# Joining blocks of 32-column matmuls in a planned two-layer transformer kernel, with an earlier start and an earlier first expert weight

## The chip, the cores and the metric

The kernel runs on one core of a Trainium2 chip. The metric is the device time of one execution in microseconds (us). The engines are named as in the profile: PE is TensorE (PEld its weight loads), DVE is VectorE, ACT is ScalarE, POOL is GpSimd, SP is SyncE, which here issues most of the DMAs.

## The reference

32 sequences of 128 tokens with 512 channels pass through two layers; `cond` gives one vector for each sequence. Everything is float32. Layer 0 is attention with 16 heads of 64 (wide: 1024 channels in all), a routing in which each of 8 experts picks its best 512 tokens of the 4096, and the experts' MLP (2048 wide). Layer 1 is attention with 16 heads of 32 and a plain MLP. Cut to what matters here:

```python
# layer 0
shift = silu(t) @ W_ada.T
h = ln(x) + shift
q, k, v = split(h @ Wqkv.T)            # q and k normed per head
o = softmax(q k^T / 8) v
x = x + o @ Wout.T
tok = x.reshape(-1, d)
gate = softmax(tok @ Wgate.T)          # 4096 x 8
vals, idx = top_k(gate.T, 512)         # per expert
y = gelu(ln(tok[idx]) @ fc1[e].T) @ fc2[e].T * vals
tok = tok.at[idx].add(y)
# layer 1
normed = adaln(x, cond)
x = x + attention(normed) @ wo.T
x = x + gelu(adaln(x, cond) @ w1.T) @ w2.T
```

## The kernel before

`fast_kernel` is one program for all of it (a second, general one stands behind it for inputs that don't fit its assumptions and doesn't run here). It does not issue instructions as it goes through the code. Each piece of work is given to a planner with `sch.op(engine, estimated us, function, w=writes, r=reads, prio, job, ...)`: an *operation*, which may be one instruction or a whole block of them. When all are known, `Sched.run` sets the order: again and again it takes the operation that can start earliest by its own estimates, and among equals the one with the lowest `prio`. A window of three jobs is open at a time. Each engine then issues its operations in that order, with waits where the data needs them. So a different estimate or one operation less can move others; `lat` is the estimated time to landing of a DMA, and `share` scales the estimated size of one.

Buffers come from pools: `row` (tiles in SBUF, the on-chip memory), `weight` (weight tiles there), `bank` (PSUM, where PE writes; eight).

- **Start.** SP issues the DMAs of `prm` (columns of parameters), `cT` (the condition), `wg` (gate weights), then the first two sequences `x` (`load_x`, L1165), `wada` (`load_w`, L1122) and six `wqkv`. ACT loads its table and makes `sT` of `cT` (L1189). DVE norms x (L336 to L339, then `xn` L1411), PE transposes it (`tpx` L1113) and multiplies `sT` with `wada` (`pa` L1197); ACT copies that (`zs_a` L1128), PE adds it up (`pu_a` L1201), DVE makes `hshift` (L1205) and `hT` (L1419), and the first projection (`pq` L1305) begins.
- **Layer 0**, `pair(g)` for 16 pairs of sequences (L1288). q, k and v come from products of half matrices in which seven products take the place of eight (`seven`, matmuls at L1346, form 128*128, a full PE array). Then `back(b, i, ...)` does the attention of sequence i of the pair: transposes of q and k (`tpq`), scores (`sc`, L1469, form 64*128), exps on ACT (`pe`, L1475), row sums of the exps with a matrix of ones (`ps`, L1485, form 128*32: the array is split into four strips of 32 columns), the outputs (`po`, L1491, form 128*32) and `oT` = `po` times the reciprocal of the sums (L1498). Ln, Exp and two DVE operations make the reciprocal (`recip`). After that the gates' logits: `gates` (L1519, form 128*32) sums `xT` times `wg` (4 matmuls) and `oT` times `ww` (8) in four strips of `pgz` (the profile counts each float32 matmul as two instructions: x8 and x16); a copy `zg`, and a small matmul `pg` with `sel` (L1523, 8 columns wide) adds the strips up. DVE copies `pg` to `lg`. `project` (L1557) multiplies `oT` with `wout`, and SP stores the result to `tok` and to `acc` in DRAM (`send`, L1579). The last 16 sequences (`LATE`) put `oT` into DRAM, and their projection (`late_projection`) comes while the routing searches its thresholds.
- **Routing and experts.** `expert_tokens` makes the list of tokens of each expert (`oh` L1712, `pi` L1732). `expert(e, after)` gathers the tokens (`xg`, POOL's indirect DMA, L1776), norms, transposes (`tpg`) and multiplies them with `fc1` (u, L1885), again with seven products for eight, for which DVE sums halves of the tokens (`tg`, L1137) and POOL halves of the weights (`s`, L1138; four sums for each of four tiles m of fc1). The tiles m = 2 and 3 of expert 0, and its fc2, wait for a small DMA, `fence`, that reads the last gathered token (L1782).
- **Layer 1**, `group(g)` for 16 groups of two sequences: transposes of the normed x (`a_..t`), q, k and v (L2251, L2297), and for each sequence the scores (`quads`, L2347, form 32*128), the exps (L2350), the row sums (`sums`, `ps`, L2358, form 128*32), the outputs (`outs`, `po`, L2364, form 128*32) and `oT`. Then the output projection (`o`, L2297) and the MLP, up (`m`, L2425) and down (`n`, L2486). PE's gaps in the attention of a group are filled with the MLP of the group before.

The lines that the change touches in `back`, cut:

```python
sch.op(PE, mm_us(D), sums, w=[ps], r=pe[0] + pe[1], prio=pa + 3, job=job)
...
pgt = pb + 41
...
sch.op(PE, mm_us(S, len(parts) // DC), gates, w=[pz], r=need, prio=pgt, job=job)
copy([zs], [pz], lambda: zs.t, lambda: pz.t, S, pgt, job)
```

and in `group`:

```python
sch.op(PE, mm_us(D), sums, w=[ps], r=pe, prio=pa + 5, job=job)
sch.op(PE, mm_us(S, 4), outs, w=[po], r=pe + [v[i]], prio=pa + 5, job=job)
```

## Time and profile before

| what | us |
|---|---|
| median of 3 runs (3240.48 to 3243.26) | 3242.57 |
| the profiled execution | 3242.52 |
| its span | 3240.5 |
| PE busy in it (share of the span) | 3199.2 (99%) |
| start, to the first `tpx` | 10.42 |
| layer 0 (to 960, the start in it) | 960 |
| routing and late projection | 126 |
| expert 0 until PE is busy again throughout (1086 to 1126) | 40 |
| the rest of the experts (to 1935) | 809 |
| layer 1 (to the end) | 1305 |

The stages are read from the trace by the lines that run in them. The first lines of the profile's page, below its sum of busy times, cut the span into 40 slices and give the busy tenths of each (9 is 90% or more) and the granted clock of PE in tenths of full speed:

```profile
PE   8999999999999899999999999999999999999999
DVE  7877776878677787756665547666666666666665
PEclk9999999999999899999999999999999999999999
```

PE's row is below 9 in the first slice (the start) and in the slice that holds the change from routing to expert 0, and PE's clock is lower there too. A line of the timeline reads: start in us, duration in us, engine, line, operation, output<-inputs, form of the array (for PE), shape, type, number of instructions, and in brackets the idle time before and what ended it. The ends of matmuls are modelled; their starts are recorded, so distances of starts are the better measure.

### The profile page before, as it was taken

The page shows a single profiled execution, that of the slowest core. Times are in us where ns is not written, and L with a number is a line of the kernel's source. Part 1 is how long each engine was busy: PE and PEld are TensorE (multiplying, and loading weights), DVE is VectorE, ACT ScalarE, POOL GpSimd, SP SyncE. Part 2 cuts the span into 40 slices and gives each one's busy share as a digit, 9 for nine tenths or more (in the row PEclk, how much of TensorE's full clock was granted, in tenths as well). Part 3 has the DMA queues.
Part 4 walks back from the last instruction along what each step waited for, and adds up shares of the span by engine and source line. Part 5 has one row for each costly group of instructions (what it writes and reads, how often), then busy time and mean ns, then how long its engine had stood idle before and what let it go on. Part 6 is the DMA issues. An engine that isn't in the chain of part 4 may idle for free. (4 is left out here: it accounts for less than half of the span.)

```text
span 3240.5 us, 55814 instructions
## 1 busy us (share of the span) xinstructions
PE 3199.2 (99%) x21786; PEld 2559.9 (79%) x21786; DVE 2242.1 (69%) x4854; ACT 959.7 (30%) x2302; POOL 705.3 (22%) x557
## 2 busy tenths in 40 slices
PE   8999999999999899999999999999999999999999
PEld 4665666555557688888888888999999999999998
DVE  7877776878677787756665547666666666666665
ACT  3333333344431122221222213333333333333332
POOL 0111111000023458766676510000000000000000
PEclk9999999999999899999999999999999999999999
DMA  4122112222125523444333463333333333333343
GB/s 173 53 78 67 63 57 76 91 83 66 51 88 195 160 86 103 119 112 116 101 103 99 146 202 103 99 99 101 100 102 102 101 102 99 98 100 101 103 137 105
DMA packets 247122, 335.39 MB, mean 103 GB/s; under 512 B 22082, under 2 KB 156738, under 8 KB 246338
## 3 DMA queue, kind: packets, MB, share of 16 engines
q1 hardware_dynamic: 239394, 314.30, 29.9%
q0 software_dynamic: 7168, 16.91, 2.8%
q8 instruction: 174, 2.85, 0.4%
q14 instruction: 98, 0.80, 0.1%
q10 hardware_dynamic: 288, 0.52, 0.1%
HBM read 277.01 MB, written 54.66 MB: 102 GB/s over the span
## 5 line engine op out<-in xcount | busy, mean ns | idle before, releaser
L2372 POOL TENSOR_TENSOR hi_t<-hi_t,inv 128x512 f32<-128x512 f32 x32 | 40.8, 1273 | 1223.7 <-DVE inv L1148 1223.7
L2436 ACT ACTIVATE m<-m,prm 128x128 f32<-128x128 f32 x512 | 162.0, 389 | 236.7 <-DVE m L2430 236.2
L1949 PE MATMUL d<-fc,h 128*128 128x256 f32 x992 | 218.9, 380 | 0.0
L1949 PEld LDWEIGHTS d<-fc,h 128*128 128x128 f32 x992 | 188.4, 190 | 24.9
L1896 ACT ACTIVATE h<-h,prm 128x256 f32<-128x256 f32 x256 | 114.9, 500 | 259.3 <-DVE h L1890 259.2
L1885 PE MATMUL u<-gT,fc 128*128 128x256 f32 x768 | 180.4, 386 | 0.8 <-ACT gT L1852 0.8
L1885 PEld LDWEIGHTS u<-gT,fc 128*128 128x128 f32 x768 | 148.6, 194 | 21.9 <-ACT gT L1852 1.2
L2430 DVE TENSOR_TENSOR m<-mu,m 128x512 f32<-128x512 f32 x128 | 87.9, 688 | 108.1 <-PE m L2425 105.2
L1312 ACT ACTIVATE sq<-qk 128x512 f32<-128x512 f32 x128 | 80.7, 632 | 232.1 <-DVE qk L1350 227.9
L2430 DVE TENSOR_TENSOR mu<-mu,m 128x512 f32<-128x512 f32 x96 | 65.9, 687 | 87.1 <-PE m L2425 87.1
L2425 PE MATMUL m<-n2a,w_s 128*128 128x128 f32 x1024 | 125.0, 276 | 0.0
L1885 PE MATMUL u<-tg,s 128*128 128x256 f32 x512 | 121.8, 381 | 2.2 <-DVE tg L1137 2.2
L2486 PE MATMUL n<-w_t,m 128*128 128x256 f32 x512 | 123.0, 380 | 0.0
L1890 DVE TENSOR_TENSOR h<-v,u 128x512 f32<-128x512 f32 x128 | 86.7, 683 | 52.0 <-PE u L1885 50.3
L2425 PE MATMUL m<-n2T,w 128*128 128x128 f32 x1024 | 119.7, 275 | 0.0
L2425 PEld LDWEIGHTS m<-n2a,w_s 128*128 128x128 f32 x1024 | 119.5, 192 | 0.0
L2425 PEld LDWEIGHTS m<-n2T,w 128*128 128x128 f32 x1024 | 118.2, 192 | 0.8
L2486 PE MATMUL n<-w_t,ms 128*128 128x256 f32 x512 | 117.6, 383 | 0.0
L1346 PE MATMUL q<-wqkv,hT 128*128 128x512 f32 x240 | 114.6, 608 | 0.5 <-DVE oT L1498 0.4
L2486 PE MATMUL n<-w,m 128*128 128x256 f32 x512 | 114.7, 383 | 0.0
L1346 PE MATMUL q<-wqkv,hsb 128*128 128x512 f32 x240 | 114.0, 597 | 0.1
L1949 PE MATMUL d<-t,hs 128*128 128x256 f32 x512 | 113.5, 379 | 0.0
(1193 smaller groups left out, 7492.3 us busy)
## 6 DMA issues: line engine op xcount, KB each, us to landing
w_t<-t2d SPq DMA_DIRECT2D x256, 256.0 KB, 3.2
w<-in_w_dram SPq DMA_DIRECT2D x192, 256.0 KB, 4.5
fc<-in_fc_dram SPq DMA_DIRECT2D x64, 512.0 KB, 4.7
fc<-in_fc_dram SPq DMA_DIRECT2D x32, 1024.0 KB, 5.6
x<-in_x_dram SPq DMA_DIRECT2D x32, 256.0 KB, 3.3
xT<-in_xT_dram SPq DMA_DIRECT2D x32, 256.0 KB, 2.7
otd<-oT SPq DMA_DIRECT2D x32, 256.0 KB, 2.1
ol<-otd SPq DMA_DIRECT2D x32, 256.0 KB, 3.7
```

Source lines behind the costliest of these rows:

```text
L1312: sch.op(ACT, act_us(D), lambda: nc.scalar.activation(sq.t, qk[i][j].t, AF.Square), w=[sq], r=[qk[i][j]], prio=pr, job=job)
L1346: nc.tensor.matmul(ps[m].t, lhs()[:, k, :], rhs[0](k), start=(k == 0), stop=(k == 1))
L1885: nc.tensor.matmul(ps[n].t[:, t, :], lhs()[:, k, t * P : (t + 1) * P], rhs.t[:, k, :], start=(k == 0), stop=(k == 1))
L1890: sch.op(DVE, dve_us(D), lambda: nc.vector.tensor_tensor(o_.t, a_.t, ps[n].t, ALU.add), w=[o_], r=[a_, ps[n]], prio=pr, job=job)
L1896: sch.op(ACT, act_us(HQ, 1), lambda t=t, c=c: nc.scalar.activation(o_.t[:, t, :], o_.t[:, t, :], AF.Gelu_apprx_tanh, bias=col("b1s", e * 1 ...
L1949: nc.tensor.matmul(ps[n].t[:, j, :], lhs[m].t[:, k, t * P : (t + 1) * P], rhs.t[:, 2 * m + k, :], start=(m == 0 and k == 0), stop=(m == NM ...
L2372: sch.op(POOL, pool_us(D), lambda inv=inv: nc.gpsimd.tensor_tensor(hi_b.t, hi_b.t, flat(inv), ALU.add), w=[hi_b], r=[inv], prio=pr + 197, ...
L2425: nc.tensor.matmul(ps[n].t[:, u, :], l1w[what].t[:, k, (NQ * q + u) * P : (NQ * q + u + 1) * P], rhs()[:, k, :], start=(k == 0), stop=(k = ...
L2430: sch.op(DVE, dve_us(D), lambda: nc.vector.tensor_tensor(o_.t, a_.t, ps[n].t, ALU.add), w=[o_, *more], r=[a_, ps[n]], prio=pq_, job=job)
L2436: sch.op(ACT, act_us(S, 1), lambda u=u, c=c: nc.scalar.activation(o_.t[:, u, :], o_.t[:, u, :], AF.Gelu, bias=col("b1", c), scale=1.0), w= ...
L2486: nc.tensor.matmul(ps[n].t, Ah[lhs][c // NQ].t[:, c % NQ, :], b_.t[:, k, :], start=(c == 0), stop=(c == 7))
```

## The change

- `prm`, `cT` and `wg` are loaded by DMAs that ACT issues instead of SP. `load_w` takes a `share`, 0.6 for `wada`, which makes the planner expect it earlier.
- In layer 0 the gates of the first sequence of a pair are no longer an operation of their own: `back` returns them as `ahead`, and they stand in one operation with the row sums of the second sequence, directly before these. The gates of the second sequence stay alone. `zg` and `pg` hold both sequences: the two small matmuls are one operation, and one DVE copy makes `lg` in place of two.
- In layer 1 the row sums and outputs of both sequences of a group are one PE operation.
- The acc stores of the last pair wait until both tok stores have landed.
- fc1's tiles 2 and 3 of expert 0 no longer wait for the fence.

```diff
@@ -1048,9 +1048,9 @@
         return const.tile(list(shape), dtype, name=name)
 
     prm = const_tile("prm", (P, NCOL))
-    nc.sync.dma_start(prm, cols)
+    nc.scalar.dma_start(prm, cols)
     cT = const_tile("cT", (P, DC, NB))
-    nc.sync.dma_start(cT, condT.rearrange("(k p) b -> p k b", p=P))
+    nc.scalar.dma_start(cT, condT.rearrange("(k p) b -> p k b", p=P))
     ident = const_tile("ident", (P, P))
     make_identity(nc, ident)
     ones_f = const_tile("ones_f", (P, 64))
@@ -1095,7 +1095,7 @@
 
     wg = const_tile("wg", (P, DC, 32))
     nc.vector.memset(wg, 0.0)
-    nc.sync.dma_start(wg[:, :, :E], wgate.rearrange("(k p) e -> p k e", p=P))
+    nc.scalar.dma_start(wg[:, :, :E], wgate.rearrange("(k p) e -> p k e", p=P))
     ww = const_tile("ww", (P, 8, 32))
     nc.vector.memset(ww, 0.0)
     wg_b, ww_b = stands(wg), stands(ww)
@@ -1116,12 +1116,12 @@
 
         return a.unsqueeze(2).to_broadcast([a.shape[0], a.shape[1], n])
 
-    def load_w(src, k0, n0, name, prio, job, lat=6.5, spare=0, r=()):
+    def load_w(src, k0, n0, name, prio, job, lat=6.5, spare=0, r=(), share=1.0):
 
         b_ = weight(name)
         sch.op(SP, 0.06, lambda: nc.sync.dma_start(
             b_.t, src[k0 : k0 + 512, n0 : n0 + 512].rearrange("(k p) n -> p k n", p=P)),
-            w=[b_], r=r, lat=lat, prio=prio, job=job, spare=spare)
+            w=[b_], r=r, lat=lat, prio=prio, job=job, spare=spare, share=share)
         return b_
 
     def copy(w, r, out_, src, n, pr, job, first=ACT):
@@ -1166,7 +1166,7 @@
 
     load_x(0)
     load_x(1)
-    wada_b = load_w(w_ada, 0, 0, "wada", -300, 0, 9.0)
+    wada_b = load_w(w_ada, 0, 0, "wada", -300, 0, 9.0, share=0.6)
 
     wqkv_b = {}
     for i, j in enumerate((4, 5, 0, 2, 1, 3)):
@@ -1381,7 +1381,10 @@
             sch.op(DVE, 0.19, lambda i=i: nc.vector.tensor_scalar(var[i].t, var[i].t, 1.0 / HD0, EPS, ALU.mult, ALU.add),
                    w=[var[i]], r=[var[i]], prio=pp + 10 + 100 * i, job=job)
             rs = st.newton(var[i], 2 * H0, f"qk_{b0 + i}", pp + 10 + 100 * i, job)
-            oT.append(back(b0 + i, i, job, lg, qk[i], v[i], rs))
+            if i == 0:
+                zs, ahead = row(f"zg_{g}", (P, 2, S)), None
+            oT_, ahead = back(b0 + i, i, job, lg, qk[i], v[i], rs, zs, ahead)
+            oT.append(oT_)
         if b0 >= NB - LATE:
             late_projection(g)
         else:
@@ -1424,7 +1427,7 @@
 
         return hT
 
-    def back(b, i, job, lg, qk, v, rs):
+    def back(b, i, job, lg, qk, v, rs, zs, ahead):
         pb = b * 100.0
         pp = pb - 50
         xt = x_b[b]
@@ -1490,7 +1493,15 @@
                     d0 = (2 * t + r) * HD0 + 32 * i
                     nc.tensor.matmul(po[i].t[g : g + 32, t, :], v[half].t[:, d0 : d0 + 32], pe[half][r].t[:, t, :],
                                      start=True, stop=True)
-        sch.op(PE, mm_us(D), sums, w=[ps], r=pe[0] + pe[1], prio=pa + 3, job=job)
+        if i == 0:
+            sch.op(PE, mm_us(D), sums, w=[ps], r=pe[0] + pe[1], prio=pa + 3, job=job)
+        else:
+
+            def gates_sums(gates0=ahead[0]):
+                gates0()
+                sums()
+            sch.op(PE, mm_us(S, 3) + mm_us(D), gates_sums, w=[ps, ahead[1]], r=pe[0] + pe[1] + ahead[2], prio=pa + 3, job=job)
+            copy([(zs, 0)], [ahead[1]], lambda: zs.t[:, 0, :], lambda p_=ahead[1]: p_.t, S, pa + 3, job)
         inv = row(f"inv_{b}", (P, 4, S))
         recip(inv, ps, pa + 4, job)
         for o_, p_, fn in zip(oT, po, (lambda: outs(0), lambda: outs(1))):
@@ -1510,7 +1521,7 @@
         parts = [(wg, k, xt_T, k) for k in range(DC)] + [(ww, k, oT[k // 4], k % 4) for k in range(8)]
         need = [xt_T, wg_b, ww_b] + oT
         pgt = pb + 41
-        pz, zs, pg = bank(f"pgz_{b}", (P, S)), row(f"zg_{b}", (P, S)), bank(f"pg_{b}", (P, E))
+        pz = bank(f"pgz_{b}", (P, S))
 
         def gates(pz=pz):
             n = len(parts) // DC
@@ -1518,17 +1529,21 @@
                 g = q % DC
                 nc.tensor.matmul(pz.t[32 * g : 32 * g + 32, :], w_[:, k, :], src.t[:, kk, :],
                                  start=(q < DC), stop=(q >= (n - 1) * DC))
-        sch.op(PE, mm_us(S, len(parts) // DC), gates, w=[pz], r=need, prio=pgt, job=job)
-        copy([zs], [pz], lambda: zs.t, lambda: pz.t, S, pgt, job)
-        sch.op(PE, mm_us(E), lambda: nc.tensor.matmul(pg.t, zs.t, sel[:, :E], start=True, stop=True), w=[pg], r=[zs, cst_b],
-               prio=pgt, job=job)
-        sch.op(DVE, 0.16, lambda: nc.vector.tensor_copy(lg.t[:, i * E : (i + 1) * E], pg.t), w=[(lg, i)], r=[pg],
-               prio=pgt, job=job)
+        if i:
+            pg = bank(f"pg_{b}", (P, 2, E))
+            sch.op(PE, mm_us(S, len(parts) // DC), gates, w=[pz], r=need, prio=pgt, job=job)
+            copy([(zs, 1)], [pz], lambda: zs.t[:, 1, :], lambda: pz.t, S, pgt, job)
+
+            def add_up():
+                for n in range(2):
+                    nc.tensor.matmul(pg.t[:, n, :], zs.t[:, n, :], sel[:, :E], start=True, stop=True)
+            sch.op(PE, mm_us(E, 2), add_up, w=[pg], r=[zs, cst_b], prio=pgt, job=job)
+            sch.op(DVE, 0.16, lambda: nc.vector.tensor_copy(lg.t, flat(pg)), w=[lg], r=[pg], prio=pgt, job=job)
         if late:
             for n in range(2):
                 sch.op(SP, 0.06, lambda n=n: nc.sync.dma_start(otd[b - NB + LATE, n], oT[n].t), w=[(otd_b, (b, n))], r=[oT[n]],
                        lat=3.0, prio=pb + 40, job=job)
-        return oT
+        return oT, (gates, pz, need)
 
 
 
@@ -1573,11 +1588,23 @@
             sch.op(DVE, dve_us(HD), lambda: nc.vector.tensor_tensor(half(i, l), ps[n].t, half(i, l), ALU.add),
                    w=[(xt[i - 1], l)], r=[ps[n], (xt[i - 1], l)], prio=pr + 1, job=job)
 
+        sends = []
+
+        def put(i, dst, db, r=()):
+            b = 2 * g + i - 1
+            sch.op(SP, 0.06, lambda: nc.sync.dma_start(dst[b * S : (b + 1) * S, :D], xt[i - 1].t),
+                   w=[(db, b)], r=[xt[i - 1], *r], lat=2.5, prio=pr + 1, job=job)
+
         def send(i):
-            b = 2 * g + i - 1
+            sends.append(i)
             for dst, db in ((tok, tok_b), (acc, acc_b)):
-                sch.op(SP, 0.06, lambda dst=dst: nc.sync.dma_start(dst[b * S : (b + 1) * S, :D], xt[i - 1].t),
-                       w=[(db, b)], r=[xt[i - 1]], lat=2.5, prio=pr + 1, job=job)
+                if db is acc_b and g == NB // 2 - 1:
+
+                    if len(sends) == 2:
+                        for i_ in sends:
+                            put(i_, acc, acc_b, r=[(tok_b, 2 * g + z) for z in range(2)])
+                else:
+                    put(i, dst, db)
 
         prod(1, A(1, 1), *B(1, 1))
         sch.op(ACT, act_us(HD), lambda: nc.scalar.copy(U[1].t, ps[1].t), w=[U[1]], r=[ps[1]], prio=pr - 1, job=job)
@@ -1792,7 +1819,7 @@
                 n0 = i * (DD // 2) + m * 2 * P
                 sch.op(SP, 0.06, lambda f=f, i=i, n0=n0: nc.sync.dma_start(
                     f.t[:, :, i, :], fc1[e][:, n0 : n0 + 2 * P].rearrange("(k p) n -> p k n", p=P)), share=0.5,
-                    w=[(f, i)], r=[fence_b] if e == 0 and m > 1 else after, lat=5.0, prio=pe_ - 900 + m, job=job, spare=2)
+                    w=[(f, i)], r=after, lat=5.0, prio=pe_ - 900 + m, job=job, spare=2)
             A = lambda i, j, f=f: f.t[:, 2 * j - 2 : 2 * j, i - 1, :]
             Sq = lambda i, g=g: g.t[:, {1: 0, 2: 1, 4: 2}[i], :, :]
             pw_ = pe_ - 700 + 10 * m
@@ -2328,7 +2355,7 @@
 
         x3 = [row(f"x3_{g}_{i}") for i in range(GB)]
         early, late = stands(None), stands(None)
-        oTs = []
+        oTs, both = [], []
         for i in range(GB):
             b = b0 + i
             pa = pr + 100 + 30 * i
@@ -2363,8 +2390,14 @@
                         h = 4 * t + r
                         nc.tensor.matmul(po.t[r * 32 : r * 32 + 32, t, :], v[i].t[:, h * HD1 : (h + 1) * HD1],
                                          pe[r].t[:, t, :], start=True, stop=True)
-            sch.op(PE, mm_us(D), sums, w=[ps], r=pe, prio=pa + 5, job=job)
-            sch.op(PE, mm_us(S, 4), outs, w=[po], r=pe + [v[i]], prio=pa + 5, job=job)
+            both.append((sums, outs, [ps, po], pe + [v[i]]))
+            if i:
+
+                sch.op(PE, 2 * (mm_us(D) + mm_us(S, 4)), lambda fs=tuple(f for x in both for f in x[:2]): [f() for f in fs],
+                       w=both[0][2] + both[1][2], r=both[0][3] + both[1][3], prio=pa + 5, job=job)
+        for i in range(GB):
+            pa = pr + 100 + 30 * i
+            ps, po = both[i][2]
             inv, oT = row(f"inv_{g}_{i}", (P, 4, S)), row(f"oT_{g}_{i}", (P, DC, S))
             recip(inv, ps, pa + 6, job)
             sch.op(DVE, dve_us(D), lambda inv=inv, po=po, oT=oT: nc.vector.tensor_tensor(
```

## Prediction

> **What bounds the kernel now.** I read the page's first two parts, then the waits of PE (TensorE), then a table of stages, then PE's timeline where the diff touches it.
>
> ```profile
> PE 3199.2 (99%) x21786; PEld 2559.9 (79%) x21786; DVE 2242.1 (69%) x4854; ACT 959.7 (30%) x2302; POOL 705.3 (22%) x557
> ```
>
> PE is busy for all but 41 us, so a change pays by making PE's own stream shorter or by closing one of its few gaps. The view of PE's waits names the large gaps (columns: who waits, for whom, total us, times, longest):
>
> ```profile
> PE tpx L1113 <- DVE xn L1411: 11.7, 2, 10.4
> PE tpg L1113 <- ACT ng_1y L320: 9.8, 1, 9.8
> PE u L1885 <- DVE tg L1137: 2.2, 2, 1.7
> PE pi L1732 <- DVE oh L1712: 1.0, 2, 0.8
> ```
>
> The first is the start, the other three the change to expert 0. The table of stages (window: length, PE busy, ..., granted PE clock) shows that elsewhere there is nothing to wait for:
>
> ```profile
> 78.00:960.00 882.00, 880.36 (x6107) 512.91 (x6106) 669.38 (x1574) 325.77 (x827) 98.08 (x86) 1.00 0.21 70
> 1097.00:1126.00 29.00, 24.98 (x121) 19.74 (x120) 22.95 (x41) 9.13 (x20) 14.74 (x12) 0.80 0.72 223
> 1935.00:3185.00 1250.00, 1249.63 (x10145) 1135.91 (x10146) 842.89 (x1949) 391.65 (x920) 40.75 (x32) 1.00 0.33 103
> ```
>
> Layer 0 has 1.6 us of idle PE in 882, layer 1 has 0.4 in 1250. There only the length of the instructions is left, and the timeline of PE (start, us, engine, line, op, tiles, array form) shows what the change aims at: each passage between the forms 128*128 and 128*32.
>
> ```profile
> 213.59 1.99 PE L1557 MATMUL w<-wout,oT 128*128 128x256 f32 x8 [0.37 <-DVE oT L1498]
> 215.51 0.43 PE L1519 MATMUL pgz<-xT,wg 128*32 128x128 f32 x8
> 215.76 0.62 PE L1519 MATMUL pgz<-oT,ww 128*32 128x128 f32 x16
> 216.31 1.99 PE L1557 MATMUL w<-wout,oT 128*128 128x256 f32 x8
> 218.14 0.29 PE L1523 MATMUL pg<-sel,zg 128*128 128x8 f32 x2
> 218.28 1.96 PE L1346 MATMUL q<-wqkv,hT 128*128 128x512 f32 x4
> 220.17 1.07 PE L1485 MATMUL ps<-pe,ones_f 128*32 128x512 f32 x8
> 221.05 1.93 PE L1491 MATMUL po<-pe,v 128*32 128x128 f32 x64
> 222.91 1.99 PE L1346 MATMUL q<-wqkv,hT 128*128 128x512 f32 x4
> 224.73 1.88 PE L1346 MATMUL q<-t,hsa 128*128 128x512 f32 x4
> ...
> 236.30 1.88 PE L1346 MATMUL q<-wqkv,hsb 128*128 128x512 f32 x4
> 238.01 1.88 PE L1346 MATMUL q<-t,hsa 128*128 128x512 f32 x4
> ```
>
> Take distances of starts, since ends are modelled: q x4 at 236.30 takes 1.71 between its like; at 222.91, just after a 128*32 block, 1.82; at 224.73, just before one, 1.81.
>
> **What the Trainium skill says.** "TensorEngine Tiling (Array Packing)", Key Properties: a change of tiling mode, not of the tile alone, drains TensorE. The trace agrees and gives the price, 0.10 us on either side. "SBUF — State Buffer", Who interferes with whom: a DVE operation with two SBUF inputs contends with GpSimd operations that read SBUF. The trace agrees: the sums `tg` (L1137) of expert 0 take 1.55 to 1.75 us while POOL adds, and a 128x512 sum of that line at 19.76, with POOL quiet, 0.68. "DMA: Bandwidth & Descriptors", Issuing engines are not separate DMA queues: issuing from several engines saves only the time that the sequencer needs for the issue. Here the three issues that leave SP occupy it from 0.81 to 2.28, 1.47 us. "TensorE: Matmul & The Clock Gate", Part 1: an idle PE falls to half clock, in windows of some 3.4 us. The records here show half clock in 1122.48–1125.89 (3.41 us).
>
> **Part 1, gates beside row sums (layer 0).** Medians over the run: wg x8 0.243 and ww x16 0.550, a block of its own with 0.096 before it and 0.104 after: 0.993 for one sequence's gates. Put right before `ps`, wg x8 stays 0.243, ww x16 is taken as 0.437 (its distance where `ps` follows it in the old trace) and `ps` itself loses the 0.025 it pays after a passage (0.883 against 0.858): 0.655. Saved 0.338. It applies to one sequence of each of 16 pairs: 5.4. The built order of instructions agrees: as many matmuls as before (11555 of the fast path, two instructions each in the profile as a rule), 128*32 blocks of layer 0 64 to 48. The two small `pg` matmuls (0.140 for x2, 0.084 on what follows) join with the other pair's; each of their matmuls costs about one weight load, so I count nothing (0 to 1.3 in all). DVE loses 16 copies, which lie under PE.
>
> The joined operation must have what both parts need. Gates of sequence 0 have waited for nothing since before; what changes is that `ps` of sequence 1 stands later by about 1.2 us of PE work (7.6 against 6.4 from the end of its scores), so its exps have more cover, and its reciprocal and `oT` come later against the projection. The 0.37 in the excerpt is such a wait; there are four of this kind in all (1.5 us). PE issues in order, so whatever stands behind the joined operation waits with it.
>
> **Part 2, layer 1.** One `ps`,`po` block per group of two sequences goes. A block costs 0.094 before, 0.025 on `ps`, 0.129 on `po` (0.987 against 0.858) and 0.104 after: 0.352, times 16 groups 5.6. The built order has 16 blocks where there were 32. In it, transposes (8) and the first six down matmuls (n) stand between the last scores and the first `ps`: about 3.5 us, where the exps of the second sequence end 2.4 us after the scores: 1.1 in hand. After the block of 3.6 us come ten n matmuls and then the output projection: `oT` of the first sequence comes 6.9 after the block's start, of the second 9.1, needed at 8.0 and 10.6. So no new stall, with 1.1 to 1.5 us in hand in each place. Four PSUM banks (ps and po of both) are now held through one block; the built order gives them to nobody who is due before.
>
> In all 63 passages of 314 go. One block of 64*128 is split more than before: −0.4. Parts 1 and 2: 5.4 + 5.6 − 0.4 = 10.6 (9 to 11.5).
>
> **Part 3, the start.** SP's three issues (prm, cT, wg) go to ACT, so x is issued 1.47 earlier; ACT's table load (1.28) comes later and sT at about 3.8 instead of 3.38, with nothing queued behind it that is due: zs_a comes at 14.29. x landed at 5.79, the norm ran without gaps to xn 9.73 and PE began at 10.42. Earlier by 1.47: about 9.0. What follows is more: the diff's share=0.6 puts `pa` (1.94 at 12.29) before the transposes in the built order. It needs wada, landed at 9.41 before, now about 8.0. So pa 8.0–9.9, transposes 9.9–11.7, pu_a 11.7–13.5; first pq 14.4 instead of 17.67. The old 0.7 wait for zs_a is filled by the transposes. Gain 3.2; I take 3.0, bounds 1.5 (half of it lost where wqkv, landed 12.12 and later, or the half clock that lasts to 23.4 here decides) and 3.6.
>
> **Part 4, expert 0.** Two of its four first-weight tiles (2 MB in four DMAs, issued 1097.14 to 1098.68 behind the fence, landed to 1109.6) lose the fence and load during layer 0; in the built order SP issues them after the first two, and POOL's eight sums stand ahead of the late projection. On SP nothing due is behind them; POOL pays the same 8 operations there, against a DVE with 25% idle (a few us, hidden). Gone is this meeting:
>
> ```profile
> 1109.53 1.55 DVE L1137 TENSOR_TENSOR tg<-gT,gT 128x512 f32<-128x512 f32 x1
> 1110.49 1.72 POOL L1138 TENSOR_TENSOR s<-fc 128x512 f32<-128x512 f32 x1
> 1111.14 1.13 PE L1885 MATMUL u<-tg,s 128*128 128x256 f32 x4 [1.65 <-DVE tg L1137]
> 1121.78 0.36 PE L1732 MATMUL pi<-val,oh 128*128 128x8 bf16 x8 [0.78 <-DVE oh L1712]
> ```
>
> Four sums of 1.55 to 1.75 become about 0.69: the stalls 1.65 + 0.54 become about 0.8 (−1.4), the stalls 0.27 + 0.78 of pi go (−1.05), and the half-clock piece of 3.41 us that follows is likely to stay away (−1.7): −4.1. Against it: the last pair's two acc stores now wait on SP for the tok stores, with b2t and the fence behind them. tok landed in 2.04 us beside acc and 2.03 before, so there is nothing to win; the acc stores (0.5 MB from 1088.4) then run beside the gathers (first 1089.30–1092.77): 0 to +0.7, taken +0.3. The 9.8 us gap stays. Sum −3.8, bounds −1 and −5.
>
> **Sum.** 10.6 + 3.0 + 3.8 = 17.4. The profiled execution took 3242.52 (span 3240.5 and 2.0 around it), which is the median of the runs (3242.57): 3225.1.
>
> **Rivals.**
> - *Only the passages pay.* The start is set by wqkv or by the clock, and expert 0 finds another late thing (gathers, fence, DMA). For it: those stages are chains of latencies, and the clock there drops in fixed pieces. Against: each named wait has its releaser in the trace. 3242.5 − 10.6 = 3232.
> - *Later oT in layer 0.* The second sequence's sums come later, and the projection waits for `oT` in every pair, not in a few. At 0.7 us in 16 pairs 11 us are given back: 3236. Against: in the built order the projection keeps q matmuls of the next pair ahead of it.
> - *A new wait in layer 1, the slower side.* The joined operation waits for the exps of both sequences, and the projection for two reciprocal chains at once. My 1.1 us in hand are worked out from old durations; if ACT, which also has the MLP's work queued there, is late by more than 1.1 + 1.09 us in each group, all 17.4 are gone. At 1.5 us of stall in each of 16 groups: 3225 + 24 = 3249.
> - *The change does little of what it says,* the order being remade by the planner: 3241. The built order speaks against it.
>
> **Chances.** Forecast 0.65 (own range 3221 to 3230), only passages 0.18, oT 0.06, new wait 0.05, little 0.06. Within 0.2% (6.5 us, about what a measurement can tell here) lie the last and the edge of the third: faster 0.89, same 0.07, slower 0.04. Unknown costs reach from 3242.5 − 9 − 1.5 − 1 = 3231 down to 3242.5 − 11.5 − 3.6 − 5 − 1.3 = 3221; with the second case at 3232 and part of the third I take 3220 to 3235.
>
> **What would show it.** 63 fewer passages in PE's timeline, some 0.34 us less for each pair of layer 0 and each group of layer 1; first pq near 14.4; tg at 0.69 and no wait of u above 1; clock 1.00 after 1126. Wrong if waits `ps <- pe` or `o <- oT` appear 16 times in layer 1, or if 78–960 is not about 5 us shorter.

## The result and the profile after

| | before | changed |
|---|---|---|
| median, 6 runs each | 3241.61 us | 3225.64 us |
| from, to | 3240.3, 3243.26 | 3224.24, 3227.05 |
| the profiled execution | 3242.52 | 3224.4 |
| its span | 3240.5 | 3222.4 |
| PE busy | 3199.2 | 3181.8 |

The ratio is 0.995, with a 95% interval from 0.9938 to 0.9961: 16 us faster, where 17.4 were forecast. Spans differ by 18.1, the two profiled executions being at the upper and the lower side of their kernels' runs.

Total and terms are two things. The lines that answer to those shown of before, first PE's waits of the changed kernel (who waits, for whom, total us, times, longest):

```profile
PE tpg L1113 <- DVE xng L1867: 11.3, 2, 11.2
PE pa L1197 <- DMA wada<-in_w_ada_dram: 9.6, 1, 9.6
PE a_0t L1113 <- DVE a_1v L339: 2.8, 1, 2.8
PE pc L1670 <- DVE junk L1668: 2.1, 4, 0.8
PE sc L1472 <- DVE qkT L1452: 1.8, 2, 1.6
PE tpq L1113 <- DVE qk L1440: 1.7, 1, 1.7
...
PE u L1912 <- DVE tg L1137: 0.8, 1, 0.8
```

The waits of `pi` are gone and those of `u` for `tg` fell from 2.2 to 0.8, as forecast. Three waits are new or grown and were not forecast: `sc` for `qkT` (0.6 before), `tpq` for `qk` (0.9 before) and `pc` for `junk` (0.5 before). They lie at the end of layer 0 and in the search for the thresholds (`pc`). The wait of `a_0t`, where layer 1 begins, is the same 2.8 in both kernels; the prediction's list leaves it out. The table of stages (window: length, PE busy, ...) with the windows of before, in which the same work now stands some us earlier:

```profile
78.00:960.00 882.00, 877.56 (x6082) 515.60 (x6081) 672.96 (x1566) 328.50 (x837) 110.55 (x98) 1.00 0.22 73
1097.00:1126.00 29.00, 28.21 (x159) 24.45 (x158) 24.46 (x42) 10.39 (x23) 7.90 (x7) 0.97 0.47 148
1935.00:3185.00 1250.00, 1249.99 (x10148) 1147.65 (x10141) 832.79 (x1937) 396.47 (x935) 40.66 (x32) 1.00 0.33 107
```

Idle PE in 78–960 is now 4.4 us where it was 1.6; in 1097–1126 it is 0.8 where it was 4.0.

The joined block of layer 0 and that of layer 1 in PE's timeline of the changed kernel:

```profile
211.61 1.88 PE L1346 MATMUL q<-t,hsa 128*128 128x512 f32 x4
213.42 0.42 PE L1530 MATMUL pgz<-xT,wg 128*32 128x128 f32 x8
213.66 0.62 PE L1530 MATMUL pgz<-oT,ww 128*32 128x128 f32 x16
214.10 1.04 PE L1488 MATMUL ps<-pe,ones_f 128*32 128x512 f32 x8
214.96 1.93 PE L1494 MATMUL po<-pe,v 128*32 128x128 f32 x64
...
2405.16 1.06 PE L2385 MATMUL ps<-pe,ones_f 128*32 128x512 f32 x8
2406.04 1.06 PE L2391 MATMUL po<-pe,v 128*32 128x128 f32 x32
2406.91 1.04 PE L2385 MATMUL ps<-pe,ones_f 128*32 128x512 f32 x8
2407.77 1.06 PE L2391 MATMUL po<-pe,v 128*32 128x128 f32 x32
```

From start to start, the gates take 0.24 + 0.44 and the `ps` behind them 0.86: the prices of the prediction. In layer 1 the first `po` takes 0.87 where each took 0.99. Over the whole trace the form of the array changes 253 times where it changed 316 times: 63 passages fewer, as forecast.

Where the two traces stand, by the start of the same work in each (us from the span's start):

| | before | changed | gained so far |
|---|---|---|---|
| first `pq` | 17.67 | 14.98 | 2.7 |
| first `sc` | 67.59 | 62.07 | 5.5 |
| first `tpg`, expert 0 | 1096.31 | 1089.53 | 6.8 |
| first `d`, expert 0 | 1158.30 | 1146.82 | 11.5 |
| first `a_0t`, layer 1 | 1912.58 | 1901.21 | 11.4 |
| end of the span | 3240.5 | 3222.4 | 18.1 |

So the start gave 5.5 (forecast 3.0), layer 0 with the routing 1.3 (forecast 5.0), expert 0 4.7 (forecast 3.8), layer 1 6.7 (forecast 5.6). Three terms came out larger, one nearly vanished. The 1.3 is a balance: from the first `sc` to the last projection PE has 5.6 less work but waits 3.0 more, and the gap before `tpg`, which the prediction took to stay at 9.8, is 11.2, 1.3 longer. The experiments ask why.

### The profile page after: what moved, and what is told of

Its sections match the earlier page's. It is cut to its first block, busy times and chain, and to the rows that moved or that the text cites. A ratio compares the mean times of both kernels' runs of the same rounds, so it can differ in the third digit from the quotient of the medians.

```text
span 3222.4 us, 55899 instructions
## 1 busy us (share of the span) xinstructions
PE 3181.8 (99%) x21786; PEld 2560.3 (79%) x21786; DVE 2230.8 (69%) x4826; ACT 964.7 (30%) x2309; POOL 712.6 (22%) x562
## 4 chain that ended last, share of the span: by engine, by line
PE 96%; DVE 3%; DMA 1%; issue 0%; ACT 0%; POOL 0%; SPq 0%; DVEq 0%; ACTq 0%; POOLq 0%
PE m L2458 12%; PE n L2519 12%; PE u L1912 12%; PE d L1976 12%; PE q L1346 11%; PE qk L2278 6%; PE w L1572 6%; PE v L1346 5%; PE v L2324 3%; PE o L2324 3%; PE sc L1472 2%; PE po L1494 2%; PE tpq L1113 1%; PE pq L1305 1%; PE sc L2374 1%; PE ps L2385 1%
## 5 line engine op out<-in xcount | busy, mean ns | idle before, releaser
L2519 PE MATMUL n<-w_t,m 128*128 128x256 f32 x512 | 116.3, 379 | 0.0
L1346 PE MATMUL q<-t,hsa 128*128 128x512 f32 x240 | 112.7, 594 | 0.0
```

The costliest lines, as they stand in the source:

```text
L1346: nc.tensor.matmul(ps[m].t, lhs()[:, k, :], rhs[0](k), start=(k == 0), stop=(k == 1))
L2519: nc.tensor.matmul(ps[n].t, Ah[lhs][c // NQ].t[:, c % NQ, :], b_.t[:, k, :], start=(c == 0), stop=(c == 7))
```

## The experiments

Each run was timed beside runs of the kernel before on the same chip. Differences are of medians; the interval of a ratio is about ±0.1%, ±3 to 4 us. The start and the clock of PE differ between executions, as shown below, so most comparisons of traces below run from one piece of work to another and leave the start out.

### Each part alone

The kernel before with one part of the change. `join1_alone`:

```diff
-            sch.op(PE, mm_us(D), sums, w=[ps], r=pe, prio=pa + 5, job=job)
-            sch.op(PE, mm_us(S, 4), outs, w=[po], r=pe + [v[i]], prio=pa + 5, job=job)
+            both.append((sums, outs, [ps, po], pe + [v[i]]))
+            if i:
...
```

> The kernel before with one part alone: row sums and outputs of both sequences of a layer-1 group in one operation. Theory A (passages as priced in the prediction): 0.352 us less in each of 16 groups, 5.6 us in all. Theory B (the two traces: a_4t to a_13t moves forward by 0.48 us per group, of which only some 0.34 lies on passages and 0.14 on transposes that wait less in the new order): 7.6 us in all, all of it in layer 1, and the distance from one group's first transpose to the next falls from 82.35 to 81.88. Rival (a new wait for the exps of both sequences): slower in layer 1, waits of ps in PE's list.

Measured: 3234.06 against 3241.21, ratio 0.9979 (0.997 to 0.9987), 7.2 us faster. From `a_4t` to `a_13t` it gains 4.28 us in nine groups, 0.476 each, as in the changed kernel. Theory B holds: 16 × 0.476 = 7.6. What the prediction had missed is a small wait that the view of PE's waits does not list, since it is PEld that waits. Before, in the timeline of PEld of that group:

```profile
2437.33 0.42 PEld L1113 LDWEIGHTS a_6t<-ident,a_6n 128*128 128x128 f32 x4 [0.32 <-DVE a_6n L2176]
```

and in the changed kernel, all eight at once and with no bracket:

```profile
2426.78 1.01 PEld L1113 LDWEIGHTS a_6t<-ident,a_6n 128*128 128x128 f32 x8
```

Before, such a wait of 0.3 us or more comes once in each of 14 groups; in the changed kernel these are gone. On PE the n matmuls ahead of it and the transposes are 0.14 us longer in the old order than the same rows elsewhere. With 0.34 for the passages that makes the 0.476. The forecast's slower rival, a wait for the exps, didn't come: no wait of `ps` or `o` in layer 1.

`gates_alone`:

```diff
-        sch.op(PE, mm_us(D), sums, w=[ps], r=pe[0] + pe[1], prio=pa + 3, job=job)
+        if i == 0:
+            sch.op(PE, mm_us(D), sums, w=[ps], r=pe[0] + pe[1], prio=pa + 3, job=job)
+        else:
...
+            sch.op(PE, mm_us(S, 3) + mm_us(D), gates_sums, w=[ps, ahead[1]], r=pe[0] + pe[1] + ahead[2], prio=pa + 3, job=job)
```

> The kernel before with one part alone: the gates of the first sequence beside the row sums of the second, pg of both in one operation. Theory A (passages): 0.338 us less in 16 pairs, 5.4 us, and nothing else. Theory B (the changed kernel's loss of 4.4 us to new waits at the end of layer 0 and in the routing belongs to this part, since it moves the later work of the last pairs): about 1 us or nothing gained. Rival: oT later for the projection in every pair, w <- oT waits in PE's list 16 times.

Measured: 3239.82 against 3241.21, ratio 0.9994 (0.9986 to 1.0003): 1.4 us, not told from none. Its waits of PE:

```profile
PE tpg L1113 <- DVE xng L1855: 12.4, 2, 12.2
...
PE tpq L1113 <- DVE qk L1440: 2.8, 1, 2.8
PE pc L1658 <- DVE junk L1656: 2.1, 4, 0.8
PE pi L1747 <- DVE oh L1727: 2.0, 3, 0.8
```

The passages are saved: from the first `sc` to the last projection the trace is 2.35 us shorter although PE idles 3.2 more in it, 5.5 less work, against 5.4 forecast. All of it is given back: 3.2 in the last pair and the search, 2.4 in a longer gap before `tpg` (12.2 for 9.8). Why the gap is longer is seen on SP, in the timeline of this kernel:

```profile
1083.66 0.32 SPq L1594 DMA_DIRECT2D tok<-xl  x1
1084.03 1.50 SPq L1594 DMA_DIRECT2D acc<-xl  x1
1085.63 0.38 SPq L1594 DMA_DIRECT2D tok<-xl  x1
```

In the new order the last pair's stores come out close together, and an acc store that occupies SP for 1.50 us stands between the two tok stores that the gathers wait for. How much of the 2.4 this order makes stays open. The second tok store also landed 2.67 us after its issue, where it took 2.04 before, and that time differs between executions: in `join1_alone`, whose layer 0 is that of before, it was 3.43, and the gap 11.3.

Why the last pair waits is seen on POOL and DVE, in their timelines:

```profile
947.50 1.27 POOL L1138 TENSOR_TENSOR s<-fc,s 128x512 f32<-128x512 f32 x1
948.73 1.27 POOL L1138 TENSOR_TENSOR s<-fc 128x512 f32<-128x512 f32 x1
```

```profile
947.62 1.19 DVE L299 TENSOR_SCALAR qk_31y<-var 128x32 int32<-128x32 int32 x1
948.85 1.20 DVE L303 SCALAR_TENSOR_TENSOR qk_31t<-qk_31y 128x32 f32<-128x32 f32 x1
950.08 1.30 DVE L305 TENSOR_TENSOR qk_31t<-qk_31t,var 128x32 f32<-128x32 f32 x1
...
952.67 0.19 DVE L305 TENSOR_TENSOR qk_30t<-qk_30t,var 128x32 f32<-128x32 f32 x1
```

The first three of DVE stand beside six of POOL's eight sums of expert 0's first weights (`s`, `fc`, L1138; 943.69 to 951.3) and take 1.19 to 1.30; the fourth stands in POOL's pause and takes 0.19. They are the reciprocal roots that the last pair's q and k wait for. Before, the eight sums stood at 947.85 to 958.0, and the last pair's roots began at 956.90: one operation met the last sum (1.13), the next took 0.19. So with the joined gates the roots begin 3.9 us after the first of these sums, where they began 9.0 after it, and meet what the old order had all but missed. The search has meetings of the same kind: each of the four waits of `pc` in the changed kernel comes within 2 us after the start of a step `cand` on DVE that took 1.03 to 1.26 beside POOL's sums of the late projection, where it takes 0.16 alone. No run moved those sums, so this part of the cause is argued and not shown.

`start_alone`:

```diff
-    nc.sync.dma_start(prm, cols)
+    nc.scalar.dma_start(prm, cols)
...
-    wada_b = load_w(w_ada, 0, 0, "wada", -300, 0, 9.0)
+    wada_b = load_w(w_ada, 0, 0, "wada", -300, 0, 9.0, share=0.6)
```

> The kernel before with one part alone: prm, cT and wg issued on ACT, and the share of wada. Theory A (prediction): the first pq comes 3.0 us earlier and the end too. Theory B (the traces): the first pq comes 2.7 earlier, and the half clock at the start ends at about 13 instead of 23.4, so that the first scores of layer 0 come 5.5 us earlier; the end by 5.5 if nothing later eats it.

Measured: 3238.98 against 3241.21, ratio 0.9992 (0.9984 to 1.0001): 2.2 us, at the edge of what can be told. In its profile the first `pq` comes 1.6 and the first `sc` 2.8 earlier, less than in the changed kernel. The start differs from one execution to another, and with it the clock. The first `pq` in the timelines of before and of the changed kernel, up to 20 us:

```profile
17.67 2.93 PE L1305 MATMUL pq<-wqkv,hT 128*128 128x512 f32 x3 [0.83 <-DVE hT L1419]
```

```profile
14.98 5.42 PE L1305 MATMUL pq<-wqkv,hT 128*128 128x512 f32 x12 [0.83 <-DVE hT L1422]
```

Behind the first one, these matmuls start 0.85 us apart before and 0.43 in the changed kernel: half clock and full clock. (The clock row of the page has no record before 23.4 and counts that time as full, so its first digit is 9; the half clock of the start shows in these distances.) The first long stretch of full clock begins at 23.4 before and at 13.1 in the changed kernel. Of the eight profiled kernels with the new start, six have it between 11.6 and 13.9 and two at 19.3 and 20.9; the five with the old start have it between 20.7 and 23.4. Their first `sc` stands at 62.5 on average (60.8 to 65.1) and at 66.4 (65.1 to 67.6). So the new start is worth some 3.9 us in the profiles, of which 2.3 is the earlier `pq` and the rest the clock, and a single execution can miss it by 2.6. The clock has a part in the 2.3 too: `pu_a`, ahead of `pq`, takes 1.92 before and 0.98 in the changed kernel. The medians show less, 2.2; where in the interval the worth lies stays open. What made `pq` earlier is told by `undo_share` below.

`fc1_alone`:

```diff
-                    w=[(f, i)], r=[fence_b] if e == 0 and m > 1 else after, lat=5.0, prio=pe_ - 900 + m, job=job, spare=2)
+                    w=[(f, i)], r=after, lat=5.0, prio=pe_ - 900 + m, job=job, spare=2)
```

> The kernel before with one part alone: the third and fourth first-weight tiles of expert 0 load without the fence. Theory A (prediction): 4.1 us less between the last projection and the first down product of expert 0, nothing lost before. Theory B: the same gain there, but POOL's eight sums now stand beside the last pair of layer 0, whose small DVE operations with two inputs grow from 0.19 to about 1.2 us, and 3 us or so are lost there; the total is near nothing to 1.5 us faster.

Measured: 3240.22 against 3241.21, ratio 0.9999 (0.999 to 1.0007): no difference. Theory B, by more than it said: in its profile 6.1 us are gained between the first `tpg` and the first `d`, and 6.0 lost between the first `sc` and the first `tpg`:

```profile
PE tpg L1113 <- DVE xng L1840: 11.5, 1, 11.5
...
PE tpq L1113 <- DVE qk L1437: 3.4, 2, 2.1
```

`tpq` waits 2.5 more than before, PE then runs at half clock from 962.77 to 966.18 (3.41 us, 1.7 lost), and the gap before `tpg` is 1.7 longer. The gain in expert 0 itself is plain over all traces: from the first `tpg` to the first `d` the five with the fence take 60.1 to 63.9 us, the nine without it 55.9 to 57.3, on average 5.5 less. Of that 3.1 is idle time of PE and 1.8 is lost at half clock.

### Each part undone

The changed kernel with one part as it was before; the edits are those above in reverse, and for the acc stores:

```diff
-                if db is acc_b and g == NB // 2 - 1:
...
-                            put(i_, acc, acc_b, r=[(tok_b, 2 * g + z) for z in range(2)])
```

> The changed kernel with one part undone: each sequence's gates an operation of their own again. Theory A (passages as priced): 5.4 us slower than the changed kernel. Theory B (what gates alone showed: the passages are saved, but 2.4 us come back as waits of tpq and sc for DVE in the last pair and 1.7 as waits of pc in the routing, and the gap before expert 0 grows): about 1.4 us slower, the waits of tpq, sc and pc at the end of layer 0 are as before (0.9, 0, 0.5).

> The changed kernel with one part undone: the third and fourth first-weight tiles of expert 0 wait for the fence. Theory A (prediction): 4.1 us slower than the changed kernel, all of it between the first u and the first d. Theory B: the same 4 to 5 us there, and 0 to 1 us faster before, since the eight sums that collide with DVE's small operations in the last pair are those of the first two tiles, which are there in both.

> The changed kernel with one part undone: the acc stores of the last pair go out at once. Prediction: no difference, or 0.3 us faster. Theory B (with the gates joined, an acc store whose issue takes 1.5 us on SP stood between the two tok stores and the second tok came 2.0 us after the first; with the change they are 0.4 apart): the first gather some 1.5 us later, the end 1.5 later.

> The changed kernel without the share of wada, so that the transposes stand before the condition product (pa) again. Theory A (prediction: the order is worth about half of the 3.2 us at the start): first pq about 1.5 us later than in the changed kernel, 16.5. Rival (wada's landing sets the first product either way): first pq within 0.5 us of it.

The changed kernel was run twice, at first (3225.64) and later on the chip of these runs (`changed_again`, 3224.63); the table has the difference to each.

| kernel | median us | to the first runs | to `changed_again` | ratio to before |
|---|---|---|---|---|
| undo_gates | 3230.46 | +4.8 | +5.8 | 0.9968 (0.9958 to 0.9979) |
| undo_fc1 | 3230.21 | +4.6 | +5.6 | 0.9969 (0.9958 to 0.9979) |
| undo_acc | 3224.16 | −1.5 | −0.5 | 0.9953 (0.9939 to 0.9966) |
| undo_share | 3226.67 | +1.0 | +2.0 | 0.9957 (0.9943 to 0.997) |

Undone, gates cost 4.8 to 5.8 and the fence 4.6 to 5.6, where alone they brought 1.4 and 1.0. Theory B of `undo_gates` is wrong in its size: without the joined gates the last pair is not as before but worse. Its waits of PE:

```profile
PE tpg L1113 <- DVE xng L1852: 10.9, 1, 10.9
...
PE tpq L1113 <- DVE qk L1437: 4.9, 2, 2.8
```

4.9 us of `tpq` and a half-clock piece from 968.1 to 971.6, as the early fc1 tiles make it in the old order (`fc1_alone`). In the order with joined gates the fc1 tiles add no such wait: `undo_fc1` has nearly the changed kernel's (`tpq` 1.8, `pc` 2.1), gains 0.9 us on it from the first `sc` to the search, and loses 5.3 between the first `u` and the first `d`. The prediction's sum for that place was 4.1.

Undoing the acc order moves the second tok store to 1.9 us after the first (0.4 in the changed kernel); the first `tpg` comes 0.7 later relative to the work ahead of it, and of that 0.2 is left at the first `d`. So that part can't be told from nothing, near the prediction, though for another reason: it repairs a delay that the joined gates bring. Theory B, 1.5 us later, did not come. Nor is the long issue bound to acc stores: in the changed kernel the second tok store itself occupies SP for 1.34 us.

Without the share the first `pq` comes at 16.57, 1.6 later than in the changed kernel, as theory A has it. But 16.57 lies within the 16.3 to 17.8 of the five kernels with the old start, and so does the first work of PE, `tpx` at 10.15 (9.9 to 10.5 there). In this one trace the order that the share sets is all of the gain, and the issues moved to ACT bring nothing by themselves. DVE shows why. Before:

```profile
2.92 0.17 DVE L1192 TENSOR_TENSOR bb<-prm 128x4 f32<-128x4 f32 x1 [1.31 <-DMA prm<-in_cols_dram]
5.81 0.69 DVE L336 BATCH_NORM_STATS2 n_0st<-x 128x6 f32<-128x512 f32 x1 [1.43 <-DMA x<-in_x_dram]
```

and in the changed kernel:

```profile
4.20 0.16 DVE L1192 TENSOR_TENSOR bb<-prm 128x4 f32<-128x4 f32 x1 [2.59 <-DMA prm<-in_cols_dram]
5.57 0.69 DVE L336 BATCH_NORM_STATS2 n_0st<-x 128x6 f32<-128x512 f32 x1
```

`x` landed 1.8 us earlier, at 3.98, but DVE did not take it up: in this program its set-up stands first and waits for `prm`, and `prm` landed 1.3 later, at 4.17. In all nine kernels with the new issues the norm begins at 5.5 to 5.7 and waits for no DMA; with the old ones it begins at 5.3 to 5.9.

### Two parts together

`gates_fc1` is the kernel before with the diffs of `gates_alone` and `fc1_alone`.

> The kernel before with two parts together: gates joined, and the third and fourth first-weight tiles of expert 0 without the fence. Theory A (each part's own worth adds): 1.4 + 1.0 = 2.4 us faster than before. Theory B (each part alone pays for one and the same disturbance of the last pair, a late qk and a late start of the search, which is paid once when both are there; undone singly from the changed kernel they are worth 4.8 and 4.6): the changed kernel's 16 less 6.8 for layer 1 and 2.2 for the start, 7 us faster.

Measured: 3236.30 against 3241.17, ratio 0.9986 (0.9979 to 0.9993): 4.9 us, twice the sum of the two alone (2.4) and less than the 7 of theory B. The interval (2.3 to 6.8) takes in the sum at its edge, so by times alone the interaction isn't proven; the traces show it. From the first `sc` to the first `d`, with the start left out, before takes 1090.7 us, the gates alone 1090.9, the fence part alone 1090.6, and both together 1085.6. Kernels that are alike in this stretch differ less: `before`, `join1_alone` and `start_alone` take 1090.3 to 1092.1. Of the waits of the last pair the kernel with both has one set and not two (`tpq` 1.8, `sc` 1.8, `pc` 2.1 in all). By medians the parts now add: 7.2 for layer 1, 2.2 for the start, 4.9 for these two, 14.3 of the measured 16.

### Where the sums of POOL stand

If POOL's sums beside the last pair's roots make the new waits, they go when the sums move. `late_sums`, on the changed kernel:

```diff
-            tt(lambda A=A, Sq=Sq: Sq(1), lambda A=A: A(2, 1), lambda A=A: A(2, 2), ALU.add, D, [(g, 1)], [(f, 1)], pw_, job, POOL, False)
+            tt(lambda A=A, Sq=Sq: Sq(1), lambda A=A: A(2, 1), lambda A=A: A(2, 2), ALU.add, D, [(g, 1)],
+               [(f, 1)] + ([] if e else [(g_b, NB // 2 - 1)]), pw_, job, POOL, False)
```

> The changed kernel, but POOL's 16 sums of expert 0's first weights wait until the last pair's gates are computed, so that none of them stands beside the last pair of layer 0. Theory (POOL's sums slow DVE's small operations from 0.19 to 1.2 us and so make the waits of tpq 1.66 and sc 1.60): both waits shrink to about 0.9 and 0.2, qk_31's and qk_30's operations are at 0.19, and the end comes 2 us earlier if the search in the routing isn't slowed. Rival (the sums then collide with the search): pc waits of more than 2.1 us in all take it back.

Measured: 3228.48, ratio 0.9963 (0.9949 to 0.9976), 2.8 more than the changed kernel's first runs and 3.9 more than `changed_again`; the intervals of the ratios overlap. The two waits are gone: up to the search the trace is 3.6 us shorter from the first `sc` on. From there to the first `tpg` it is 6.6 longer, so the rival takes the gain back with more:

```profile
PE pc L1670 <- DVE junk L1668: 6.7, 5, 2.4
```

A half-clock piece of 3.41 us, at 997.12, follows. The search is a chain of small DVE operations and suffers as the roots did; on DVE, beside the sum of POOL from 993.89 to 995.29:

```profile
994.31 1.03 DVE L1674 SCALAR_TENSOR_TENSOR cand<-drop,cand 128x1 int32<-128x1 int32 x1
```

So the sums must stand between the two. `sums_after_norms`:

```diff
             rs = st.newton(var[i], 2 * H0, f"qk_{b0 + i}", pp + 10 + 100 * i, job)
+            if g == NB // 2 - 1:
+                last_rs.append(rs)
...
-            tt(lambda A=A, Sq=Sq: Sq(1), lambda A=A: A(2, 1), lambda A=A: A(2, 2), ALU.add, D, [(g, 1)], [(f, 1)], pw_, job, POOL, False)
+            tt(lambda A=A, Sq=Sq: Sq(1), lambda A=A: A(2, 1), lambda A=A: A(2, 2), ALU.add, D, [(g, 1)],
+               [(f, 1)] + ([] if e else last_rs), pw_, job, POOL, False)
```

> The changed kernel, but POOL's 16 sums of expert 0's first weights wait for the reciprocal roots of the last pair (so that they stand between those and the search, not beside either). PE's order is the same. Theory: no operation of qk_30 and qk_31 on DVE above 0.3 us, the waits of tpq (1.66) and sc (1.60) in the last pair shrink to under 0.5 together, pc waits stay at about 2.1: 2.5 us faster than the changed kernel, 3223. Rival (the order of the two roots on DVE, not POOL, makes the waits): both waits stay over 1 us and the time is that of the changed kernel.

> The changed kernel once more, to compare with the three others on the same chip, and to see how much its start and its half-clock pieces differ between two executions: 3224 to 3227 us; first scores of layer 0 at 62 if the early rise of the clock at the start is the change's own, up to 3 us later if it is chance.

Measured on one chip: 3221.04 (3219.64 to 3226.53) for `sums_after_norms`, 3224.63 (3223.86 to 3226.32) for the changed kernel again; ratios to before 0.9944 (0.993 to 0.9957) and 0.9949 (0.9936 to 0.9963). One of the slow operations in the changed kernel:

```profile
942.97 1.20 DVE L303 SCALAR_TENSOR_TENSOR qk_31t<-qk_31y 128x32 f32<-128x32 f32 x1
```

The timelines of DVE, POOL and PE in `sums_after_norms`:

```profile
940.39 0.18 DVE L299 TENSOR_SCALAR qk_31y<-var 128x32 int32<-128x32 int32 x1
940.60 0.19 DVE L303 SCALAR_TENSOR_TENSOR qk_31t<-qk_31y 128x32 f32<-128x32 f32 x1
940.83 0.19 DVE L305 TENSOR_TENSOR qk_31t<-qk_31t,var 128x32 f32<-128x32 f32 x1
```

```profile
950.53 1.27 POOL L1138 TENSOR_TENSOR s<-fc 128x512 f32<-128x512 f32 x1
```

```profile
946.40 1.04 PE L1113 MATMUL tpq<-ident,qk 128*128 128x128 f32 x8
947.27 1.88 PE L1347 MATMUL v<-tv,hsa 128*128 128x512 f32 x4
949.08 2.06 PE L1475 MATMUL sc<-qkT,qkT 64*128 64x128 f32 x32
```

The same operations that took 1.2 take 0.19, and `tpq` and `sc` of the last pair wait for nothing; the order of PE is that of the changed kernel, and the order of the two roots on DVE too, so POOL's sums made the waits. A new one of 1.4 (`pgz` for `oT`) takes part of it back: at the first product of the search 1.9 us are left. The 3.6 between the medians is more than that, and the intervals overlap. This kernel is the fastest one run here; by how much it beats the changed kernel is open between nothing and some 4 us. (From the first `sc` to the end its trace is 3.2 and 3.9 us shorter than the two of the changed kernel. Of this, 1.9 and 2.2 arise up to the first `tpg`; the rest lies in expert 0 and layer 1, where this trace has less time at half clock.) `changed_again` shows what repeats: its first `sc` at 61.59, the waits of the last pair 2.0 and 1.6, its median within 1.0 of the first six runs.

## Why the prediction was right, and where it wasn't

The total was right, 3225.1 for 3225.64, and its terms were not.

- *Part 1 (5.0 after the extra split): the price was right, its net not.* Each passage cost what the rows of before said (5.5 less work in `gates_alone`, 5.6 in the changed kernel). The step that failed is that this saving was taken to arrive whole. The argument for it, that the exps of the joined operation "have more cover", looked at exps and `oT`, and not at the reciprocal roots of the last pair, where there is no next pair to fill PE and where POOL's sums stand. The waits there and in the search took 3.0 back. "The 9.8 us gap stays" failed too: it is 11.2, which took 1.3 more. The prediction's own sign of being wrong for layer 0, less than about 5 us gained, came.
- *Part 2 (5.6): under by 1.1 to 2.* The passages are 0.34 per group; 0.14 came from transposes that no longer wait for `a_..n`, a wait that only PEld's rows show. The changed kernel's trace shows 6.7 and not 7.6; the half-clock piece at the start of layer 1 is 6.83 us long in it and 3.41 before. Over all traces layer 1 is 7.0 shorter with the joined blocks.
- *Part 3 (3.0): near in the first `pq`, 2.7 for 3.2, but by other steps.* That `x` and `wada`, issued 1.5 earlier, would be used 1.5 earlier failed: the norm began 0.2 earlier, and `wada` landed at 9.44 (9.41 before), so that `pa` began at 9.57 and not at 8.0, 0.9 before PE's old start. That the share's order fills the wait for `zs_a` was right (0.7). The rest came from `pu_a` at full clock, 0.9, which was not foreseen; that the 2.7 lie so near is luck. Nor was it foreseen that half clock would end 10 us earlier, or that it differs between executions; 5.5 in the profile and 2.2 in the medians lie on either side of 3.0.
- *Part 4 (3.8): near, and rather under.* 4.7 in the changed kernel, 4.6 to 5.6 by undoing, 5.5 over all traces. All four named rows came out: `tg` at 0.68, `u` waits 0.8, `pi` none, and no half-clock piece after 1098.6 until layer 1. Its sentence that POOL's work in layer 0 is "hidden" held nearly so in the order with joined gates, where it cost 0.9 (`undo_fc1`); alone, it was paid in full (`fc1_alone`).
- *The acc stores: not told from nothing,* near the 0.3 taken.
- *Rivals.* "Only the passages pay" is out for expert 0. The slower rival in layer 1 didn't come. Later `oT` in layer 0 came in `sums_after_norms` alone, where `pgz` waits 1.4 us for it, and not in 16 pairs.

That the errors cancelled (start, layer 1 and expert 0 gave 4.5 more in the profile, layer 0 3.7 less) is luck.

## What to carry to other kernels

- Where PE is busy throughout, count the passages between array forms and price each from distances of starts in the trace; two blocks of one form belong together. But look at the last round of a loop on its own: no next round covers it there, and a planner that is given shorter blocks shifts what meets what.
- A part that is worth little alone may be worth its full price beside another, when both cause one and the same stall: undo parts singly from the whole as well as adding them singly, before one is thrown away.
- Put an engine's bulk work, such as POOL's sums, where no chain of small operations of the engine that it slows is on the path: between two chains, not beside either. Here the waits of the first chain went with that; how much time it brings lies within the noise.

## What was not expected of the hardware

- DVE operations on 128x32 elements took up to 1.30 us beside POOL's sums of 128x512 and 0.18 to 0.19 without, six times as long, and ones on 128x1 (`cand`) up to 1.26 and 0.16 without. The search's 128x256 operation `junk`, which reads one tile and sums it up, stayed at 0.48 in all 30 steps, in `late_sums` too.
- The first long stretch of full clock of PE began anywhere from 11.6 to 23.4 us, up to 9 us apart in kernels with the same start, with pq matmuls 0.43 and 0.85 us apart. Half-clock pieces between full ones lasted 3.41 us or a multiple of it (6.83, 13.65, 17.07).
- A store of 256 KB occupied SP's queue for 1.34 us (a tok store, changed kernel) or 1.50 (an acc store, `gates_alone`) at its issue, where the others around it took 0.32 to 0.45.
